# Two graph layers on one core: keys on partitions, unshifted softmax, heads in groups of the array, two batches woven

**Chip, cores, metric.** One core of one Trainium2 chip. The metric is the device time in microseconds of one execution of the whole program; less is better. Engines: PE is TensorE, PEld its weight loads, DVE VectorE, ACT ScalarE, POOL GpSimd.

## The reference, cut

Sixteen graphs of N = 1024 nodes and D = 256 features. The adjacency is 0 or 1 with about 3% ones, although layer 0 accepts edge types 1 to 5.

```python
# layer 0: 4 heads x 64, logits chosen by edge type
h = einsum('bnd,hde->bhne', x, W)
for t in range(5):
    weight += (adj == t + 1) * (e_src[:, :, t, :, None] + e_dst[:, :, t, None, :])
weight = where(adj == 0, -1e9, leaky_relu(weight, 0.01))
dst = einsum('bhij,bhje->bhie', softmax(weight), h) + bias
x = layernorm(x + head_layernorm(relu(dst) + h))
# layer 1: 8 heads x 32, self-attention over the edges, then an MLP 256 -> 1024 -> 256
q = layer_norm(x)                                 # queries, keys and values alike
scores = where(adj > 0, einsum('bhqd,bhkd->bhqk', q, q) / sqrt(32), -inf)
y = x + einsum('bhqk,bhkd->bhqd', softmax(scores), q)
x = layernorm(x + y + gelu(layer_norm(y) @ W1 + b1) @ W2 + b2)
```

## The kernel before

Queries lie on partitions. A head's logits for 128 queries form a 128 x 1024 tile; its row maximum falls out of the masking pass, the exponential gives the row sum, and then the weights must be turned over on PE, 128 x 128 at a time, since a product contracts over partitions and the values have keys there. The cuts are marked `...`.

```python
def logits0(k, hd, es3, ed3, mt, neg0, sums):        # layer 0, 128 queries, one head
    w = two.tile([P, N], F32, name="w")
    for t in range(T):                               # five edge types
        e = ps_s.tile([P, N], F32, name="ps")
        for n in range(NH):
            nc.tensor.matmul(e[:, cols], sel[:, r : r + 1].to_broadcast(...), ed3[:, cols], ...)
            nc.tensor.matmul(e[:, cols], es3[:, ...], sel[:, r : r + 1].to_broadcast(...), ...)
        ...
            nc.vector.copy_predicated(w, mt[:, t, :], e)
    ...
    nc.vector.tensor_tensor_reduce(p, p, neg0, 1.0, -3e38, OP.add, OP.max, mx)
    nc.scalar.activation(p, p, AF.Exp, bias=nmx, scale=1.0, accum_out=sums[:, hd : hd + 1])

def logits1(k, hd, nT, neg1, sums, mxs):             # layer 1: 32 of 128 array rows in use
    c, q = divmod(hd * HD, P)
    for n in range(NH):
        nc.tensor.matmul(s[:, cols], nT[q : q + HD, c, k * P : (k + 1) * P], nT[q : q + HD, c, cols], ...)
    ...

def turn(k, hd):                                     # both layers: weights to keys on partitions
    for q in range(BPH):
        nc.tensor.transpose(pt[:, q, :], p[:, j * P : (j + 1) * P], ident)
    nc.scalar.copy(pT[:, g * BPH : (g + 1) * BPH, :], pt)

def products(k, hd):                                 # both layers: 32 or 64 columns per weight load
    for j in range(NB):
        nc.tensor.matmul(acc[k][:, hd, :], pT[:, j, :], values[:, j, ...], ...)
```

The three stages are woven over the heads, but batches run strictly one after the other.

## Time and profile before

| | before |
|---|---|
| time, median of 3 runs | 17754.5 us (17746.7 to 17767.2) |
| one batch, 17751.8 / 16 | 1109 us |
| PE busy / mean granted clock | 88% / 0.618 |
| DVE, ACT, POOL busy | 41%, 22%, 25% |

A high share of busy PE is not a full array: PE counts as busy while a product uses 32 of its 128 rows, or runs at half clock.

### The profile page before, as it was taken

Reading aid. Unit: us, or ns where it says so; the run is one execution under the profiler, and the core shown is the slowest. Engines: PE = TensorE matmul, PEld = TensorE weight load, DVE = VectorE, ACT = ScalarE, POOL = GpSimd, SP = SyncE. Lnnn points to the kernel's source line nnn. Section 1 sums busy time; section 2 is a strip of 40 time slices with the busy share of each in tenths; the row PEclk is TensorE's granted clock in tenths of the full one; section 3 lists DMA queues with packets and bytes.
Section 4 is the critical chain, followed back from the end, with each engine's and each line's share of the span. In section 5 each row is a group of like instructions: output and inputs, shape, how many; then the busy total and the mean of one; then the engine's idle time right before and its main releaser. Section 6 shows DMA issues by size and latency. Waiting matters only on the chain.

```text
span 17751.8 us, 142034 instructions
## 1 busy us (share of the span) xinstructions
PE 15601.4 (88%) x56064; PEld 10318.6 (58%) x56064; DVE 7284.9 (41%) x12747; ACT 3990.1 (22%) x6880; POOL 4354.5 (25%) x2950
## 2 busy tenths in 40 slices
PE   7988979889798897988979889798897988979889
PEld 4655646556465564655646556465574655646556
DVE  6245162451624516245162451624516245162441
ACT  1222212222122221221212222122221221212222
POOL 5123041230412304123041230412304123041220
PEclk7566575665756657566575665756657566575665
DMA  0000000000000000000000000000000000000000
GB/s 25 3 8 8 3 10 3 8 8 3 10 3 8 8 4 9 3 8 8 4 9 3 8 8 4 9 3 8 7 5 8 3 9 6 4 9 0 9 2 3
DMA packets 59372, 113.19 MB, mean 6 GB/s; under 512 B 7249, under 2 KB 42065, under 8 KB 58705
## 3 DMA queue, kind: packets, MB, share of 16 engines
q1 hardware_dynamic: 53504, 100.68, 1.7%
q8 instruction: 442, 7.24, 0.2%
q10 hardware_dynamic: 5200, 3.42, 0.1%
q14 instruction: 226, 1.84, 0.0%
HBM read 87.31 MB, written 16.78 MB: 6 GB/s over the span
## 4 chain that ended last, share of the span: by engine, by line
PE 68%; POOL 14%; DVE 14%; issue 3%; DMA 1%; ACT 1%; ACTq 0%; DVEq 0%; POOLq 0%
PE po L367 21%; PE ps L298 20%; PE pt L386 14%; DVE w L260 7%; POOL mt L231 6%; PE ps L247 3%; PE ps L250 3%; PE po L347 2%; PE ps L339 2%; POOL neg L233 2%; DVE w L258 2%; POOL neg L234 1%; DMA ak<-in_adj_dram 1%; POOL na L160 1%; POOL o L286 1%
## 5 line engine op out<-in xcount | busy, mean ns | idle before, releaser
L247 PE MATMUL ps<-ed,sel 96*128 96x512 bf16 x5120 | 2589.7, 506 | 1601.8 <-DVE mv L153 530.7
L303 DVE CUSTOM_DVE_ANT_0 p<-ps,neg 128x1024 f32<-128x1024 f32 x1024 | 1253.7, 1224 | 6374.6 <-PE ps L298 6374.6
L367 PEld LDWEIGHTS po<-nrm,pT 128*128 128x128 f32 x16384 | 3562.1, 327 | 200.8 <-issue 200.8
L298 PE MATMUL ps<-fT 32*128 32x512 f32 x4096 | 3617.9, 1089 | 28.5 <-DVE mxs L303 21.1
L367 PE MATMUL po<-nrm,pT 128*128 128x32 f32 x16384 | 3497.3, 387 | 0.0
L386 PEld LDWEIGHTS pt<-ident,p 128*128 128x128 f32 x12288 | 2409.2, 219 | 1652.2 <-issue 1377.3
L387 ACT COPY pT<-pt 128x512 f32<-128x512 f32 x3072 | 1772.9, 585 | 6423.3 <-PE pt L386 6421.5
L260 DVE COPY_PREDICATED w<-mt,ps 128x1024 f32<-128x1024 uint8 x2048 | 2644.5, 1291 | 1136.6 <-PE ps L250 1109.4
L386 PE MATMUL pt<-ident,p 128*128 128x128 f32 x12288 | 2918.2, 413 | 81.1 <-ACT p L267 80.8
L250 PE MATMUL ps<-sel,es 96*128 96x512 bf16 x5120 | 2584.9, 505 | 0.0
L231 POOL TENSOR_SCALAR mt<-ak 128x1024 uint8<-128x1024 int32 x640 | 1772.9, 2784 | 2535.1 <-DVE w L260 2511.8
L250 PEld LDWEIGHTS <-es 96*128 96x128 bf16 x5120 | 625.2, 122 | 2346.7 <-issue 2186.8
L322 POOL TENSOR_TENSOR o<-o,x 128x256 f32<-128x256 f32 x128 | 92.8, 725 | 7614.6 <-DVE nmx L305 7531.5
L298 PEld LDWEIGHTS ps<-fT 32*128 32x128 f32 x4096 | 1062.3, 313 | 942.6 <-issue 813.8
L367 PEld LDWEIGHTS po<-h,pT 128*128 128x128 f32 x8192 | 1368.0, 240 | 209.8 <-ACT pT L387 77.2
L267 ACT ACTIVATE p<-p,nmx 128x1024 f32<-128x1024 f32 x512 | 588.2, 1149 | 3674.9 <-DVE nmx L266 3667.7
L367 PE MATMUL po<-h,pT 128*128 128x64 f32 x8192 | 1317.0, 318 | 0.3 <-ACT pT L387 0.3
L306 ACT ACTIVATE p<-p,nmx 128x1024 f32<-128x1024 f32 x1024 | 1177.3, 1150 | 237.8 <-DVE nmx L305 236.4
L247 PEld LDWEIGHTS <-sel 96*128 96x128 bf16 x5120 | 680.6, 133 | 936.5 <-issue 533.4
L145 POOL TENSOR_TENSOR r<-v,mhalf 128x1 f32<-128x1 f32 (+1 forms) x640 | 427.7, 668 | 1926.5 <-DVE v L143 1905.9
L262 DVE SCALAR_TENSOR_TENSOR p<-w 128x1024 f32<-128x1024 f32 x512 | 734.2, 1434 | 17.7
L264 DVE CUSTOM_DVE_ANT_0 p<-p,neg 128x1024 f32<-128x1024 f32 x512 | 710.6, 1388 | 1.1
(90 smaller groups left out, 7645.9 us busy)
## 6 DMA issues: line engine op xcount, KB each, us to landing
ak<-in_adj_dram SPq DMA_DIRECT2D x128, 512.0 KB, 3.6
xb<-in_x_dram SPq DMA_DIRECT2D x16, 1024.0 KB, 5.3
out_dram<-z SPq DMA_DIRECT2D x128, 128.0 KB, 1.7
w_sb<-in_L_gnn_W_dram ACTq DMA_DIRECT2D x2, 1024.0 KB, 8.3
w_sb<-in_L_gnn_W_dram ACTq DMA_DIRECT2D x2, 128.0 KB, 6.4
g_r<-in_L_gnn_gamma_dram ACTq DMA_DIRECT2D x2, 128.0 KB, 6.7
be_r<-in_L_gnn_beta_dram ACTq DMA_DIRECT2D x2, 128.0 KB, 6.6
bias_r<-in_L_gnn_bias_dram ACTq DMA_DIRECT2D x1, 128.0 KB, 6.3
```

Source lines behind the costliest of these rows:

```text
L231: nc.gpsimd.tensor_scalar(mt[:, t, :], ak, float(t + 1), None, op0=OP.is_equal)
L247: nc.tensor.matmul(e[:, cols], sel[:, r : r + 1].to_broadcast([3 * G, P]), ed3[:, cols], start=True, stop=False)
L250: nc.tensor.matmul(e[:, cols], es3[:, k * P : (k + 1) * P], sel[:, r : r + 1].to_broadcast([3 * G, HALF]), start=False, stop=True,)
L260: nc.vector.copy_predicated(w, mt[:, t, :], e)
L262: nc.vector.scalar_tensor_tensor(p, w, 0.01, w, op0=OP.mult, op1=OP.max)
L264: nc.vector.tensor_tensor_reduce(p, p, neg0, 1.0, -3e38, OP.add, OP.max, mx)
L298: nc.tensor.matmul(s[:, cols], nT[q : q + HD, c, k * P : (k + 1) * P], nT[q : q + HD, c, cols], start=True, stop=True)
L303: nc.vector.tensor_tensor_reduce(p, s, neg1[:, k, :], SCALE1, -3e38, OP.add, OP.max, mx)
L306: nc.scalar.activation(p, p, AF.Exp, bias=nmx, scale=1.0, accum_out=sums[:, hd : hd + 1])
L367: nc.tensor.matmul(acc[k][:, hd, :], pT[:, j, :], values[:, j, hd * width : (hd + 1) * width], start=j == 0, stop=j == NB - 1,)
L386: nc.tensor.transpose(pt[:, q, :], p[:, j * P : (j + 1) * P], ident)
L387: nc.scalar.copy(pT[:, g * BPH : (g + 1) * BPH, :], pt)
```

## The change

Its intent: weights come into being with keys already on partitions, so nothing is turned over; the row sum comes out of the value products; nothing is shifted by a maximum, since a test of the data allows that; heads share the array by groups of 32 rows or columns; and layer 1 of one batch is emitted together with layer 0 of the next. It is nearly a rewrite, so the diff is cut to its core.

```diff
-    # selector products, copy_predicated per type, masked max, Exp with row sum, transposes
+    def layer0(b):                                   # keys on partitions
+        for hd in range(H0):
+            acc = ps([P, NH, HALF], "z")
+            for j in range(NB):
+                g = ring.tile([P, N], F32, name="g")
+                nc.vector.scalar_tensor_tensor(      # the whole weight: max(al, gam) * adj^T
+                    g, al[:, hd, :], gam[:, j, hd : hd + 1], at[:, j, :], op0=OP.max, op1=OP.mult)
+                for n in range(NH):                  # 64 values and a column for the row sum
+                    nc.tensor.matmul(acc[: HO + 1, n, :], ha[:, j, hd, :], g[:, ...], ...)
+                yield
+            ...                                      # divide, relu, residual, norm of the head
+    def layer1(b):
+        def scores(n, c, j):
+            pair = [ps([P, 2, HALF]) for _ in range(HC // 2)]
+            for hh in range(HC):                     # 4 heads in 4 row groups
+                q = hh * HD
+                nc.tensor.matmul(pair[hh // 2][:, hh % 2, :],
+                    nT[q : q + HD, c, j * P : (j + 1) * P], nT[q : q + HD, c, cols], start=True, stop=False)
+            for hh in range(HC):                     # adds -32768 where no edge is
+                nc.tensor.matmul(pair[hh // 2][:, hh % 2, :], negI, zt[:, j, cols], start=False, stop=True)
+            ...
+                nc.scalar.activation(w, s, AF.Exp, scale=SCALE1)
+        def values(acc, c, j, ws):
+            for part in range(2):                    # 4 values, then 4 row sums, in 4 column groups
+                for hh in range(HC):
+                    nc.tensor.matmul(acc[hh * HD : (hh + 1) * HD, part, :],
+                        nrm[:, j, f : f + HD] if part == 0 else ones, ws[hh // 2][:, hh % 2, :], ...)
+        ...                                          # norm, MLP, final norm, for each half of the queries
+    for b in range(B):
+        gens = [(layer1(b), 1)]
+        if b + 1 < B:
+            gens.append((layer0(b + 1), 1))
+        weave(*gens)                                 # one step of each in turn
+        if b + 2 < B:
+            weave((prepare(b + 2), 1))               # adjacency and x transposed, h, exponentials
+    ...
+    with tc.If(failed > 0):                          # tests of adjacency and logits failed
+        general_path(inner)                          # the old method
```

A **step** below is one turn of layer 1's inner loop: four scores, four mask products, two exponentials, four values and four row sums, all for one block of 128 keys, one half of the queries and four heads. A batch has 32. The order in which PE executes is set when the program is built: a scheduler may place an instruction that was emitted later into a place where the earlier ones are still waiting.

## The prediction

> **What bounds the kernel now.** I read the page's busy shares and clock first, then a table by stage of one batch (16 alike, 17751.8 / 16 = 1109 us each), then the groups kept apart by shape, then the timeline of TensorE inside a stage.
>
> ```profile
> PE 15601.4 (88%) x56064; PEld 10318.6 (58%) x56064; DVE 7284.9 (41%) x12747; ACT 3990.1 (22%) x6880; POOL 4354.5 (25%) x2950
> PEclk7566575665756657566575665756657566575665
> PE 68%; POOL 14%; DVE 14%; issue 3%; DMA 1%; ACT 1%; ACTq 0%; DVEq 0%; POOLq 0%
> ```
>
> PE is busy 88% of the time and holds 68% of the chain that ended last, at a granted clock of 0.5 to 0.7. Bytes do not matter (6 GB/s).
>
> ```profile
> 499.50:1082.00 582.50, 557.53 (x1802) 393.16 (x1802) 114.74 (x293) 152.86 (x267) 53.15 (x53) 0.50 0.01 2
> 100.00:499.50 399.50, 310.16 (x1244) 186.54 (x1243) 276.76 (x407) 69.06 (x119) 200.71 (x117) 0.66 0.03 8
> 1082.00:1150.00 68.00, 66.39 (x249) 44.96 (x248) 14.82 (x46) 14.86 (x26) 18.28 (x16) 0.94 0.09 30
> ```
>
> Columns: stretch, length, then busy us of PE, PEld, DVE, ACT, POOL, and the clock. The first is layer 1's attention: PE 96% busy, clock 0.50 throughout. The second is layer 0's: PE 78% and DVE 69% busy, trading waits. The third is the MLP and the next batch's preparation, at 0.94.
>
> ```profile
> L298 PE MATMUL ps<-fT 32*128 32x512 f32 x4096 | 3617.9, 1089 | 28.5 <-DVE mxs L303 21.1 <-ACT fT L168 7.4
> L367 PE MATMUL po<-nrm,pT 128*128 128x32 f32 x16384 | 3497.3, 387 | 0.0
> L386 PE MATMUL pt<-ident,p 128*128 128x128 f32 x12288 | 2918.2, 413 | 81.1 <-ACT p L267 80.8
> L250 PE MATMUL ps<-sel,es 96*128 96x512 bf16 x5120 | 2584.9, 505 | 0.0
> L194 PE MATMUL ps<-fT,w_sb 128*128 128x512 f32 x256 | 112.5, 592 | 0.0
> L262 DVE SCALAR_TENSOR_TENSOR p<-w 128x1024 f32<-128x1024 f32 x512 | 734.2, 1434 | 17.7
> L306 ACT ACTIVATE p<-p,nmx 128x1024 f32<-128x1024 f32 x1024 | 1177.3, 1150 | 237.8 <-DVE nmx L305 236.4
> L315 DVE RECIPROCAL rinv<-edge 128x8 f32<-128x8 f32 x128 | 26.0, 203 | 4.4
> L272 DVE RECIPROCAL rinv<-sums 128x4 f32<-128x4 f32 x128 | 21.5, 168 | 21.9 <-ACT p L267 21.9
> ```
>
> For matmuls divide busy time by count (means contain the pipeline's tail). L298's loop makes 2048 products but leaves 4096 records: a float32 matmul is two passes. A float32 pass of 512 columns takes 112.5/256 = **0.44 us** at full clock (L194) and 3617.9/4096 = **0.88 us** at half (L298); I call the first T. A bf16 matmul of 512 takes 0.505 at mixed clock, so I take half of T, 0.22, at full clock. A float32 transpose takes 2918.2/12288 = 0.24 us.
>
> ```profile
> 801.05 3.78 PE L298 MATMUL ps<-fT 32*128 32x512 f32 x4
> ```
>
> The four passes of one head's scores fill 3.78 us one after another, on 32 of 128 rows. Bursts of this kind are longer than a clock window yet never raised the clock in 582 us, whereas a run of 128-row float32 products did within microseconds of the MLP's start.
>
> **What the Trainium skill says.** "TensorE: Matmul & The Clock Gate", Part 1: the array runs at half clock until activity in a window of about 3.4 us releases it; the trace agrees on the two levels (0.50, 1.00; T doubles). Same page, Part 3: matmuls on different row or column groups overlap, but matmuls keep strict order. The kernel before has no neighbouring products in different groups, so its trace shows nothing of this. "TensorEngine Tiling (Array Packing)", Key Properties: changing the tiling mode drains the array; not visible before either, layer 1's sums leave room for about 0.1 us a switch. "VectorE: DVE Perf Modes", First, the fixed hardware budget: reciprocal is iterative, repeat count 8; the rows agree: (203 - 168)/4 = 8.75 ns per element against about 1.1 for other work.
>
> **The change, part by part** (per batch, full clock).
>
> *Removed.* All 768 weight transposes and their 1773 us of copies on ACT; the narrow products (L367, 32 or 64 columns per weight load, 3497 + 1317 us); all 640 selector products (5175 us); DVE's five predicated passes and masked maxima; GpSimd's masks. These are most of 15601 us of PE. The general path is a branch not taken for this data (edges 0/1, small logits): I charge it nothing.
>
> *Layer 1, added.* 32 steps (2 query halves, 2 head groups, 8 key blocks), each with 4 float32 scores on four row groups, 4 bf16 mask products over the whole array, and 8 float32 value products (4 values, 4 row-sum replicas by ones) on four column groups, 512 columns each. Serial this is 8T + 2T + 16T = 26T. With overlap and strict order the two passes of one product still follow each other on their own group, and the next product's first pass can run only beside the previous one's second: n products take n + 1 passes. So 5T + 2T + 9T = 16T = 7.0 us; four mode switches make **7.3 us** (estimate). Times 32: 234 us, against 582 before. Two Exps of 1.15 us per step on ACT hide under 7.3 us.
>
> *Layer 0.* 64 float32 products of 512 columns (K 128, M 65): 64 x 0.88 = 56 us, woven beside layer 1 but on the same PE, so it adds. Its DVE pass is 32 x 1.43 = 46 us, hidden.
>
> *MLP.* 64 products of 512: 56 us, much as before. *Transposes* of results, norms and MLP output: 96 x 0.24 = 23 us.
>
> *Waits.* Layer norm before each MLP is a DVE chain of 10 to 18 us (reciprocal of 512 elements alone about 4.5 us); the first has layer 0 steps beside it, the second has none left: 8 + 14 us. Each head end of layer 0 copies its one PSUM accumulator out before the transposes: 4 x 2 us. Together 30 us (estimate).
>
> *Preparation* is emitted after the woven stretch, not in it. Eight adjacency loads through two buffers, 64 bf16 transposes, 2048-element copies on ACT (about 2 us), an 8192-element ACT pass of about 8 us that the built order puts between the two x^T copies, 16 products of 264 columns (32 passes x 0.24) and 16 of 512 (14 us): 57 us, half of it PE.
>
> *Sum:* 234 + 56 + 56 + 23 + 30 + 57 = 456 us. Fifteen of these 6840; last batch without layer 0 and preparation about 340; prologue about 200 (one preparation, and layer 0 of batch 0 with nothing woven). **About 7400 us.** DVE comes to some 145 us a batch, ACT 125: neither binds.
>
> **Rivals.**
> *The clock stays at half.* If activity is counted by cells in use, the steps (two groups of four at a time, 65 columns of 128 in layer 0) keep the array about half used, and 0.50 could persist as in layer 1 before. For it: the K=32 bursts that never raised the clock. Against: values and layer 0 use all 128 rows, and the built order keeps them back to back for 13T. Steps and layer 0 would double: 456 + 234 + 56 = 746, about **11000 us**.
> *Full overlap:* if passes of all four groups run at once, a step is 2T + 2T + 4T = 3.5 us; 456 - 122 = 334 a batch, about **5500 us**. Against it: the strict order.
> *No overlap* for two-pass products, 26T = 11.4 us: 587 a batch, about **9500 us** at full clock, beyond 15000 at half. Against: the order of instructions is plainly written for overlap, and the ones products would make no sense serially.
> *Waits win:* head tails on DVE's in-order queue (about 7 us of small work each), the norm chains and a preparation slowed by the casting loads could add 50 us a batch, about **8200 us**.
>
> **Range and chances.** I give the strict-order overlap 0.6, full overlap 0.2, none 0.2, and a clock mostly at full 0.65. The median lies a little above 7400 because most errors lengthen it: **7800 us**. The range, 5600 to 11600, goes from full overlap to half clock with strict order. Even no overlap at half clock would only approach 17754. Faster by over 2%: 0.98; within 2%: 0.01; slower: 0.01.
>
> **What would show it.** Right: about 450 us per batch; a woven step of about 9 us (7.3 + two layer 0 products); score passes in neighbouring row groups starting about T apart, pairwise overlapping; clock above 0.9 in woven stretches; some 50 to 60 us of half-idle PE between them; DVE under 40%. Wrong: a clock near 0.5 in woven stretches; four scores starting together or eight passes strictly in line; DVE or ACT ending most of PE's waits inside steps; preparation much over 60 us.

## The result

| | before | after |
|---|---|---|
| time, median of 4 runs each | 17760.85 us | 5627.2 us (5621.9 to 5631.7) |
| ratio | | 0.3168 (0.3163 to 0.3172) |
| PE busy, us | 15601.4 | 4825.3 |
| mean granted clock | 0.618 | 0.911 |

Ratios here and below are the mean time of one kernel's fast runs over that of the other's of the same rounds, so not quite the ratio of the medians. All outputs are right.

The page of the kernel after, the lines of busy time, of the clock over the span in 40 slices, and of the shares of the chain that ended last:

```profile
PE 4825.3 (86%) x22273; PEld 1764.0 (31%) x22273; DVE 2006.9 (36%) x3361; ACT 1836.4 (33%) x1952; POOL 323.0 (6%) x295
PEclk9898998989989899898989989899898998989998
PE 66%; issue 12%; DVE 11%; DMA 5%; ACT 4%; POOL 2%; ACTq 0%; POOLq 0%; DVEq 0%
```

PE still bounds the kernel, but at 0.8 to 0.9 and more of full clock in every slice, with a third of the busy time. GpSimd has left the chain nearly altogether (14% before, 2% now).

Where a batch spends its time, kernel after, two consecutive windows (stretch, length, then busy us of PE, PEld, DVE, ACT, POOL, the clock, the share of DMA and GB/s). The first runs from the start of one batch's woven stretch to its end, the second is the preparation that follows:

```profile
1952.04:2246.62 294.58, 268.02 (x1241) 87.88 (x1240) 112.34 (x184) 90.50 (x100) 14.70 (x9) 0.94 0.02 6
2246.62:2300.20 53.58, 35.08 (x152) 22.86 (x152) 12.61 (x24) 24.28 (x23) 5.38 (x9) 0.71 0.29 49
```

A batch takes 348 us where 456 were predicted. The clock and the preparation (53.6 us against 57) are close to the prediction, so nearly all of the difference of 108 us lies in the woven stretch: 294.6 us against 456 - 57 = 399. One woven step there, timeline of PE (start, duration, line, tile, shape, instructions):

```profile
2310.89 1.14 PE L365 MATMUL ps_s<-nT 32*128 32x512 f32 x8
2311.96 1.04 PE L373 MATMUL ps_s<-zt,negI 128*128 128x512 fp8e4 x4
2312.93 1.07 PE L385 MATMUL ps_a<-w,nrm 128*32 128x512 f32 x8
2313.81 1.04 PE L385 MATMUL ps_a<-w,ones 128*32 128x512 f32 x8
2314.78 1.93 PE L286 MATMUL ps_z<-g,ha 128*65 128x512 f32 x4
```

From start to start, layer 1's own work takes 2314.78 - 2310.89 = 3.9 us, not 7.3, and layer 0's two products (four passes) the expected 1.9. Eight score passes occupy 1.07 us. One pass alone takes T = 0.44, so eight in line would take 3.5 us and two rounds of four at once 0.88. The same row in the kernel before needed 3.78 us for four passes in line, at half clock.

Cut still finer, windows that count only the score products (length, PE busy, matmul records of the window, then the same of the weight loads and the clock):

```profile
2310.90:2311.00 0.10, 0.10 (x4) 0.10 (x5) 1.00 0.00 0
2311.40:2311.60 0.20, 0.20 (x8) 0.00 (x0) 1.00 0.00 0
```

Four records are in flight within the first tenth of a microsecond, and some 0.5 us later eight touch one window: the first four ending, the second four beginning. That is four heads side by side, twice, which the prediction had listed under "wrong".

Groups of instructions of the kernel after, from the page (busy us, mean ns of one, idle time before them and what ended it):

```profile
L365 PE MATMUL ps_s<-nT 32*128 32x512 f32 x4096 | 681.3, 645 | 15.7 <-ACT w L377 13.8
L385 PE MATMUL ps_a<-w,nrm 128*32 128x512 f32 x4096 | 545.0, 604 | 0.0
L286 PE MATMUL ps_z<-g,ha 128*65 128x512 f32 x2048 | 1029.3, 633 | 99.6 <-DVE g L282 60.5
L445 PE MATMUL ps_s<-fT,w_sb 128*128 128x512 f32 x1024 | 529.0, 651 | 44.7 <-ACT hid L452 25.9
L456 PE MATMUL ps_a<-hid,w_sb 128*128 128x512 f32 x1024 | 460.3, 592 | 0.0
L406 DVE RECIPROCAL den<-ps_a 128x512 f32<-128x512 f32 x64 | 214.8, 3356 | 311.9 <-PE ps_a L385 311.9
L377 ACT ACTIVATE w<-ps_s 128x1024 f32<-128x1024 f32 x1024 | 995.4, 1020 | 1520.9 <-PE ps_s L373 1520.9
```

The scores are the same 4096 passes as before: 3617.9 us then, 681.3 now. A factor of two of that is the clock, the rest is the four row groups. Only 13.8 us of PE's waits before them are for an exponential, so the exponentials hide. Per batch, layer 0's products take 1029.3 / 16 = 64 us and the MLP (529.0 + 460.3) / 16 = 62 us, together as much as the 32 steps of layer 1's attention, 32 x 3.9 = 125 us.

What still costs: PE is idle for 5628.2 - 4825.3 = 803 us. Much of it looks like this, the second norm before an MLP, timeline of PE (in brackets the idle time and what ended it):

```profile
2199.41 1.76 PE L416 MATMUL ps_s<-ident,u 128*128 128x128 f32 x7 [0.60 <-DVE u L408]
2210.64 1.97 PE L433 MATMUL ps_s<-ident,t 128*128 128x128 f32 x8 [9.47 <-DVE t L429]
```

PE waits 9.5 us for DVE's norm because no layer 0 product is left; before the first MLP of a batch 16 passes of layer 0, 8.95 us of them, fill the same place. The experiments ask two things: why a step takes 3.9 us, and whether the weaving and the rest of the change pay.

### The profile page after: what moved, and what is told of

Same layout as the page of the kernel before. It is cut to its first block, busy times and chain, and to the rows that moved or that the text cites. A ratio compares the mean times of both kernels' runs of the same rounds, so it can differ in the third digit from the quotient of the medians.

```text
span 5628.2 us, 51957 instructions
## 1 busy us (share of the span) xinstructions
PE 4825.3 (86%) x22273; PEld 1764.0 (31%) x22273; DVE 2006.9 (36%) x3361; ACT 1836.4 (33%) x1952; POOL 323.0 (6%) x295
## 4 chain that ended last, share of the span: by engine, by line
PE 66%; issue 12%; DVE 11%; DMA 5%; ACT 4%; POOL 2%; ACTq 0%; POOLq 0%; DVEq 0%
PE ps_a L385 16%; PE ps_z L286 14%; PE ps_s L365 10%; PE ps_s L373 8%; PE ps_s L445 5%; PE ps_a L456 4%; PE ps_s L262 4%; DMA ab<-in_adj_dram 4%; DVE den L406 3%; PE ps_s L239 2%; ACT zt L272 2%; POOL r L184 1%; DVE st L192 1%; POOL r L320 1%; PE ps_s L216 1%
## 5 line engine op out<-in xcount | busy, mean ns | idle before, releaser
L377 ACT ACTIVATE w<-ps_s 128x1024 f32<-128x1024 f32 x1024 | 995.4, 1020 | 1520.9 <-PE ps_s L373 1520.9
L286 PE MATMUL ps_z<-g,ha 128*65 128x512 f32 x2048 | 1029.3, 633 | 99.6 <-DVE g L282 60.5
L282 DVE SCALAR_TENSOR_TENSOR g<-al,gam,at 128x1024 f32<-128x1024 f32 x512 | 647.3, 1282 | 1302.4 <-PE ps_z L286 1300.1
L365 PE MATMUL ps_s<-nT 32*128 32x512 f32 x4096 | 681.3, 645 | 15.7 <-ACT w L377 13.8
L445 PE MATMUL ps_s<-fT,w_sb 128*128 128x512 f32 x1024 | 529.0, 651 | 44.7 <-ACT hid L452 25.9
L385 PE MATMUL ps_a<-w,ones 128*32 128x512 f32 x4096 | 548.7, 592 | 0.0
L385 PE MATMUL ps_a<-w,nrm 128*32 128x512 f32 x4096 | 545.0, 604 | 0.0
L373 PE MATMUL ps_s<-zt,negI 128*128 128x512 fp8e4 x2048 | 533.9, 382 | 0.0
L286 PEld LDWEIGHTS ps_z<-g,ha 128*65 128x65 f32 x2048 | 266.4, 144 | 782.6 <-issue 675.4
L456 PE MATMUL ps_a<-hid,w_sb 128*128 128x512 f32 x1024 | 460.3, 592 | 0.0
L406 DVE RECIPROCAL den<-ps_a 128x512 f32<-128x512 f32 x64 | 214.8, 3356 | 311.9 <-PE ps_a L385 311.9
L216 PE MATMUL ps_s<-identb,ab 128*128 128x128 bf16 x1024 | 113.2, 279 | 214.1 <-DMA ab<-in_adj_dram 182.2
```

What stands on the lines that cost most here:

```text
L282: nc.vector.scalar_tensor_tensor(g, st["al"][:, hd, :], st["gam"][:, j, hd : hd + 1], st["at"][:, j, :], op0=OP.max, op1=OP.mult)
L286: nc.tensor.matmul(acc[: HO + 1, n, :], st["ha"][:, j, hd, :], g[:, n * HALF : (n + 1) * HALF], start=j == 0, stop=j == NB - 1,)
L365: nc.tensor.matmul(pair[hh // 2][:, hh % 2, :], nT[q : q + HD, c, j * P : (j + 1) * P], nT[q : q + HD, c, cols], start=True, stop=False,)
L373: nc.tensor.matmul(pair[hh // 2][:, hh % 2, :], negI, zt[:, j, cols], start=False, stop=True)
L377: nc.scalar.activation(w, s, AF.Exp, scale=SCALE1)
L385: nc.tensor.matmul(acc[hh * HD : (hh + 1) * HD, part, :], nrm[:, j, f : f + HD] if part == 0 else ones, ws[hh // 2][:, hh % 2, :], start=j ...
```

## The experiments

| run | edit, against | median us | ratio to before |
|---|---|---|---|
| e1_values_by_group | values and sums head by head | 5636.8 | 0.3171 |
| e2_scores_serial | each score followed by its mask | 8421.9 | 0.4738 |
| e3_unwoven | layers emitted one after the other | 5353.4 | 0.3011 |
| e4_prepare_woven | preparation woven too | 5925.0 | 0.3332 |
| e5_sums_on_dve | e3, row sums gathered by DVE | 5464.8 | 0.3075 |
| e6_four_adj_buffers | e3, 4 adjacency buffers | 5359.4 | 0.3015 |
| e7_no_general_path | branch left out | 5621.3 | 0.3164 |
| e8_weave_two_to_one | two steps of layer 1 to one of layer 0 | 5347.9 | 0.3008 |
| e9_x_early_adj4 | e8 + e6 + x loaded in pieces | 5329.1 | 0.3002 |
| e10_sums_on_dve_two_to_one | e5 + e8 | 5318.2 | 0.2996 |
| e11_sums_dve_x_early | e10 + x loaded in pieces | 5259.3 | 0.2962 |

Intervals of the ratios are within 0.0007 of the values shown, of e2's within 0.0013.

### e1: does the order across groups bind?

The theory of the prediction, strict order, allows overlap only between neighbouring products in different groups. Its rival: each group goes through its own products in order and knows nothing of the others. If strict order holds, putting a head's values and sums next to each other, both in the same group, must cost much.

```diff
-                for part in range(2):
-                    for hh in range(HC):
+                for hh in range(HC):
+                    for part in range(2):
```

> The eight value products of a step are issued group by group (values of head 0, ones of head 0, values of head 1, ...) instead of first the values of all four column groups, then the ones. Same products, same result. T is one float32 pass of 512 columns, 0.44 us; in the changed kernel the sixteen passes take 4T = 1.77 us. Theory G (a product waits until its own column group is free, and no later product starts before it): head 1's first product starts together with head 0's second, so the eight products take five product times, 10T = 4.4 us; 2.6 us more in each of 512 steps, about 6980 us. Theory R (the single passes keep a strict order, and only the passes of neighbouring products on different groups were put side by side): 13T = 5.7 us, about 7660 us. Theory Q (each group has its own queue): nothing changes, about 5630 us.

Measured: 5636.8 us against 5627.2, no difference worth a name. One could suspect that the scheduler undid the edit. The order of the built program goes nrm (the values), ones (the row sums), nrm, ones through the four heads. For this text the kernel of e1 was built once more; the instructions compiled for PE stand in that order too, with the two passes of a product next to each other. The trace shows another order. Windows of e1, first those of the ones products alone, then those of the nrm products alone (length, PE busy, records, weight loads, DVE, clock):

```profile
2311.50:2311.90 0.40, 0.00 (x0) 0.10 (x4) 0.00 (x0) 1.00 0.00 0
2311.90:2312.20 0.30, 0.00 (x0) 0.06 (x4) 0.00 (x0) 1.00 0.00 0
2312.20:2312.50 0.30, 0.27 (x4) 0.15 (x4) 0.00 (x0) 1.00 0.00 0
```

```profile
2311.30:2311.50 0.20, 0.15 (x4) 0.15 (x8) 0.00 (x0) 1.00 0.00 0
2311.50:2311.90 0.40, 0.40 (x8) 0.03 (x2) 0.00 (x0) 1.00 0.00 0
```

All four heads' nrm products start within 0.2 us, though three of them stand behind a ones product in the program, and no ones product runs before 2312.2, 0.9 us later, when its own group is free. So a product waits for its own group, not for earlier products of other groups. That settles the step: scores 2T, masks 2T, values and sums 4T, together 3.52 us, and the switches between groups of rows, the whole array and groups of columns. Why the chip lets the groups run apart is not something these runs show.

### e2: one group at a time

```diff
                     )
-                for hh in range(HC):
                     nc.tensor.matmul(pair[hh // 2][:, hh % 2, :], negI, zt[:, j, cols], start=False, stop=True)
```

A mask product uses all 128 rows and now stands between any two scores; in the timeline below each score runs alone.

> Each head's score product is followed at once by its full-array mask product, so that no two score products can overlap. Same products, same result. If the overlap of the four row groups is what made the steps short: scores take 8T instead of 2T, 2.6 us more, and six more switches of mode at about 0.1 us, so 3.2 us more in each of 512 steps, about 7290 us. If the waits on ScalarE and VectorE set the steps and the overlap was worth little: under 6000 us. The granted clock should fall below the 0.91 of the changed kernel if a single 32-row group counts as little activity, and stay if any streaming counts.

Measured: 8421.9 us, 2795 more than after, a good deal beyond what was expected. The direction shows that the overlap of the row groups is what made the scores cheap: the scores' busy time went from 681.3 to 2654.2 us, in the page of e2:

```profile
L365 PE MATMUL ps_s<-nT 32*128 32x512 f32 x4096 | 2654.2, 731 | 0.0
```

The size needs a second cause. Timeline of PE in e2, a score and its mask product, at two places:

```profile
3408.80 1.12 PE L365 MATMUL ps_s<-nT 32*128 32x512 f32 x2
3409.86 0.39 PE L372 MATMUL ps_s<-zt,negI 128*128 128x512 fp8e4 x1
...
3427.54 2.07 PE L365 MATMUL ps_s<-nT 32*128 32x512 f32 x2
3429.54 0.61 PE L372 MATMUL ps_s<-zt,negI 128*128 128x512 fp8e4 x1
```

From its start to the next start the same pair takes 1.38 us at 3408 and 2.54 us at 3427. Windows of one microsecond, during the first pair and after the last pair of its step (length, busy us of the engines, clock):

```profile
3409.00:3410.00 1.00, 1.00 (x3) 0.19 (x2) 1.00 (x1) 0.00 (x0) 0.00 (x0) 1.00 0.00 0
3415.00:3416.00 1.00, 1.00 (x12) 0.36 (x8) 0.00 (x0) 0.48 (x1) 0.00 (x0) 0.50 0.00 0
```

PE is busy in every microsecond, yet some 5.5 us after single scores and masks began at 3408.8 the clock drops to 0.50 for some 3 us, and the values that run then take nearly twice as long: over the whole run nrm and ones together go from 1094 to 1694 us. The delay is not a constant: singles begin again at 3422.2, the clock falls 2.7 us later and stays at 0.50 for some 10 us. The mean clock is 0.798 against 0.911. So products on 32 of 128 rows, one at a time with masks between them, do not hold the clock up here (whether the few rows or the many switches matter was not separated), which fits the scores of the kernel before, at 0.50 throughout. The prediction's worry that half-used arrays might keep the clock down was right for one row group alone and wrong for four at once.

### e3: does the weaving pay?

```diff
-            weave(*gens)
+            for g in gens:
+                weave(g)
```

> Layer 1 of a batch and layer 0 of the next are emitted one after the other instead of woven. If the weave hides the waits (Exp of ScalarE behind only 1.8 us of value products, about 0.7 us exposed in 32 steps; four head ends of layer 0 at about 9 us; the norm of layer 0, 20 us; the first norm before the MLP, 10 us): about 90 us more per batch, about 7000 us, and a lower clock. If the matmuls set the time wherever they stand: under 5950 us.

Measured: 5353.4 us, 5% **faster** than the woven kernel. That lies within the second theory's "under 5950", but neither theory had foreseen a gain. Timeline of PE in e3, around the second norm before an MLP, the place shown above for the kernel after:

```profile
2042.55 6.17 PE L286 MATMUL ps_z<-g,ha 128*65 128x512 f32 x14
...
2061.33 1.09 PE L433 MATMUL ps_s<-ident,t 128*128 128x128 f32 x8 [0.22 <-DVE t L429]
```

And one line of its view of waits (total us, times, longest):

```profile
PE ps_s L433 <- DVE t L429: 20.4, 6, 9.6
```

Layer 0's products (L286) now stand where the norm before an MLP made PE wait: its wait is 0.22 us here (between the lines left out PE waits 5 us for layer 0's own head end). The group "PE waits for DVE's t" falls from 161 us in 17 waits to 20 us in 6. The scheduler puts layer 0 there by itself, because emitted after layer 1 it is taken only where layer 1 has nothing ready. The weave of one to one did the opposite: it spent layer 0 in steps that PE fills without help: counted from mask to mask in the traces, 384 steps of e3 hold no layer 0 product and take 3.89 us (median), and 240 steps of the kernel after hold two and take 5.76, so the two cost their full 1.87 us there. The count closes: PE's idle time goes from 803 to 678 us (span 5349.8 less 4671.6 busy), and its busy time falls by 154 us for the same 22273 instructions; 125 + 154 = 279 us is the difference of the two spans. The mean clock rises from 0.911 to 0.929, which by itself would take 4825 x (1 - 0.911 / 0.929) = 93 us off the busy time (estimate); what the rest is was not separated.

### e8: half the weave

This tests the reading of e3 from the other side. If layer 0 is worth most as filler, two steps of layer 1 to one of layer 0 should leave enough of it for the second norm.

```diff
-            gens = [(layer1(b), 1)]
+            gens = [(layer1(b), 2)]
```

> The changed kernel with the weave at two steps of layer 1 to one of layer 0, so that half of layer 0 is left when the second norm and MLP of layer 1 come. Theory of the filler (layer 0 is worth most beside the norms and the start of the next preparation, and the one-to-one weave has used it up by then, in steps that TensorE fills anyway): close to the version emitted layer by layer, 5350 to 5450 us. Rival (the gain of that version is from something else, as fewer changes of shape inside the steps): between, 5480 to 5600 us.

Measured: 5347.9 us, as e3. The wait for DVE's t is down to 19 us in 2 waits. The filler theory stands.

### e4: weave the preparation as well

Preparation takes 54 us per batch at a clock of 0.71, a third of it idle. Emitted with layer 0 of its batch beside layer 1 of the one before, it might hide.

```diff
+        def ahead(b):
+            yield from prepare(b)
+            yield from layer0(b)
...
-                gens.append((layer0(b + 1), 1))
+                gens.append((ahead(b + 1), 1))
             weave(*gens)
-            if b + 2 < B:
-                weave((prepare(b + 2), 1))
```

It also needed a buffer of its own for the MLP's input, and for that room layer 0 got three buffers for its weights in place of four.

> The preparation of the next batch is woven beside layer 1 as well, ahead of its layer 0 (its own buffer for the MLP's transposed input; three instead of four buffers for g to make room). In the changed kernel the preparation stands alone, 53 us per batch of which TensorE idles about 20. If those idle times are filled: 15 x 20 = 300 us less, about 5330 us. If the preparation takes the two PSUM buffers of the scores and stalls them as much as it saves: 5550 to 5700 us.

Measured: 5925.0 us, 5% **slower** than after. Timeline of PE in e4:

```profile
2008.43 0.72 PE L350 MATMUL ps_z<-ident,nrm 128*128 128x128 f32 x2 [22.15 <-DVE nrm L344]
...
2025.55 1.13 PE L366 MATMUL ps_s<-nT 32*128 32x512 f32 x4 [0.46 <-ACT at L218]
```

Two things go wrong. The end of layer 0, its norm, now has nothing beside it, and PE waits 22 us for it. And the preparation takes the two PSUM buffers of the scores: in the second line the scores wait for ACT's copy of an adjacency tile, and only four of the eight passes are there. Both show in the totals: PE's waits for nrm go from 26.6 us in the kernel after to 404.7, the scores' busy time from 681.3 to 893.8 us, while the waits for adjacency loads nearly go (from 182.2 to 10.4). How the net 298 us divide, and what the three buffers cost, was not separated.

### e5, e10: row sums by DVE

The ones products repeat the same sum 32 times over. DVE, at 37%, can add the weights over the eight key blocks, so that one round of ones products replaces eight. e5 does so on e3, e10 on e8's weave. Layer 0's weights had to go down to two buffers.

```diff
+            def add(wsum, before, ws, j):
+                for i in range(HC // 2):
+                    nc.vector.tensor_add(wsum[:, i], before[i] if j == 1 else wsum[:, i], ws[i])
...
                         if before is not None:
+                            add(wsum, before, ws, j)
                             values(acc, c, j - 1, before)      # 4 values only
...
+                    sums(acc, wsum)                            # 4 ones products, once
```

> Built on the version emitted layer by layer (5353 us). VectorE adds the exponentials of the eight key blocks (two additions of 1024 columns, about 1.22 us each by the rows of that shape, in 7 of 8 steps), and one round of ones products replaces eight. TensorE loses 7/8 of the 533 us of ones products, 466 us; a step falls from 3.9 to 3.0 us, and the additions (2.4 us) fit beside it. If TensorE still sets the end: 4890 to 5000 us. If VectorE's in-order queue (then some 3070 us busy) becomes the wait, because layer 0's g and the norms stand behind the additions: above 5200 us. It also has two buffers for g instead of four, to make room.

Measured: 5464.8 us, 2% slower than e3. A step should have lost 0.97 us; it went from 3.9 to 3.69. Timeline of PE in e5, one step:

```profile
2036.12 1.04 PE L374 MATMUL ps_s<-zt,negI 128*128 128x512 fp8e4 x4
2037.09 1.06 PE L385 MATMUL ps_a<-w,nrm 128*32 128x512 f32 x8
2038.08 1.80 PE L366 MATMUL ps_s<-nT 32*128 32x512 f32 x8
```

The scores now spread over 1.80 us instead of 1.14. In the view of waits, their weight loads wait for ACT's exponentials, which free the scores' two PSUM buffers:

```profile
PEld ps_s L366 <- ACT w L378: 547.6, 879, 1.2
PE ps_s L230 <- DMA xb<-in_x_dram: 313.8, 15, 21.1
```

(total us, times, longest.) ACT's two exponentials of this step run from 2036.76 to 2038.70, and the second pair of scores starts at 2038.75. Masks, two exponentials one after the other, then the next scores: this round takes 3.69 us (the median of 384 steps), and most of the ones products' 0.97 us had stood in its shadow. The total of the first line alone would not show that: it is 403.3 us in e3 too, whose steps lose nothing by it. The second line is work that e5 no longer hides, the load of x: 169.8 us in e3. The median time lies in the range of the rival, DVE's queue, and layer 0's weights do come late (82.0 us of PE's waits; e3 lists none); whether DVE's additions or the two buffers cause this was not separated.

> Row sums on VectorE as in the earlier run, but with the two-to-one weave. Theory (without the ones products a step of 3.0 us of TensorE work is shorter than the round from masks through two Exps back to the score buffers, 3.7 us; layer 0 products fill it in every second step): 0.2 us saved in one half of the steps and 0.9 in the other, 5348 - 280 = about 5070, up to 5150 us. Rival (VectorE's additions delay g and the norms, whatever stands in the steps): above 5350 us.

Measured: 5318.2 us, ratio 0.2996 against 0.3008 of e8, so 0.4% faster and far short of what was expected. Steps with two layer 0 products take 4.90 us (5.76 in e8), those without 3.69 (3.89 in e8), so a filled step does save the 0.9 us expected. But the trace has only 105 such filled steps of 512, not half: the scheduler puts most of layer 0 elsewhere. In the other steps the exponentials still hold the scores back (the scores' busy time is 884.3 us against 682.5 in e8), PE waits 175.6 us for x (115.5 in e8), and layer 0's weights now come late from a DVE that is 57% busy (205.0 us of waits by weight loads, 111.5 by products).

### e6, e9, e11: the loads of the preparation

In e3 PE still waits 165 us for adjacency tiles and 170 us for x. e6 gives the adjacency four buffers for two (and layer 0's weights three for four). e9 adds the weave of e8 and loads x in two halves where they are used, and again per head for the residual, so that its buffer no longer has to be held until layer 0 ends. e11 is e10 with x loaded that way.

```diff
-            xb = st["xb"] = one.tile([P, NB, D], F32, name="xb")
-            nc.sync.dma_start(xb, x[b].rearrange("(k p) d -> p k d", p=P))
...
             for c in range(DC):
+                xb = one.tile([P, NB, P], F32, name="xb")
+                nc.sync.dma_start(xb, x[b].rearrange("(k p) d -> p k d", p=P)[:, :, c * P : (c + 1) * P])
...
             for hd in range(H0):
+                xh = two.tile([P, NB, HO], F32, name="xh")
+                nc.sync.dma_start(xh, x[b].rearrange("(k p) d -> p k d", p=P)[:, :, hd * HO : (hd + 1) * HO])
```

> Built on the version emitted layer by layer (5353 us): four buffers for the adjacency loads instead of two (three for g instead of four). There TensorE idled 165 us until such a load had landed. If those waits end the preparation: 100 to 150 us less, about 5230 us. If other waits stand close behind them (the load of x, the copies of ScalarE, the 7 us pass over zt): 5320 to 5350 us.

> The two-to-one weave (5348 us) with both loads of the preparation made early: four buffers for the adjacency blocks, and x loaded in two halves for the transposes and again per head for the residual, so that no load waits until layer 0 has used x up (the run with four adjacency buffers alone gained nothing: the wait for x grew from 170 to 318 us). If the loads are what the preparation waits for: the 160 us for adjacency and 115 us for x go, 5100 to 5200 us. If ScalarE's copies and the pass over zt stand behind them: 5280 to 5350 us.

> The run before with x loaded in halves and again per head. In the version with sums on VectorE emitted layer by layer TensorE idled 314 us for x. If that wait is real and nothing stands behind it: 100 to 250 us below the run before. If the adjacency loads, still in two buffers, end the wait: within 40 us of it.

Measured: e6 5359.4 us, nothing gained on e3; e9 5329.1, which by the ratios (0.3002, 0.2997 to 0.3007, against 0.3008, 0.3003 to 0.3013, on another chip) is not told apart from e8; e11 5259.3, 59 less than e10 on the same chip, and the best of all. One line of the view of waits of e6:

```profile
PE ps_s L231 <- DMA xb<-in_x_dram: 317.8, 15, 21.7
```

With the adjacency early (its wait falls from 165 to 6.8 us), PE comes to x sooner and waits for that: 317.8 us instead of 170. In e9 both waits are lower than in e8, from which it differs (x 97 us after 115.5, adjacency 68.4 after 162.4), but the end of layer 0's norm holds up the transposes behind it: 101.6 us by products (44.0 in e8) and 118.4 by weight loads (39.6). Against e10, e11 halves the wait for x (82.7 us after 175.6); the adjacency, with only two buffers, stays (128.1 after 134.2). Each cure moves PE to the next thing that is late. What would remain if all of them were cured at once was not tried.

### e7: is the branch free?

```diff
-    failed = nc.values_load(bad_i[0:1, 0:1], min_val=0, max_val=1)
-    with tc.If(failed > 0):
-        with ExitStack() as inner:
-            general_path(inner)
```

> The changed kernel without the general path and its branch (the tests are still computed). The prediction charged the branch nothing: 5605 to 5630 us against 5627. If the path not taken costs anything (code to fetch, constants kept): over 1% less, under 5570 us.

Measured: 5621.3 us (5611 to 5630) against 5627.2 (5622 to 5632): ratios 0.3164 (0.3159 to 0.3169) and 0.3168 (0.3163 to 0.3172), not told apart. The branch that is not taken costs nothing measurable.

## Why the prediction was right or wrong

The time, 5627 us, lies just inside the range of 5600 to 11600 and the direction was given 0.98; but the reckoning of 7400 was 1800 us too long, and nearly all of it is one term. That the range holds the result, by 27 us, is no merit of the mechanism believed in: its lower end had been set for the rival with full overlap.

**The failed step** is "with overlap and strict order ... n products take n + 1 passes", which made a step 5T + 2T + 9T = 16T, 7.3 us with its switches. The runs show 2T + 2T + 4T = 8T, 3.5 us, and 3.9 with the switches: e1 shows that the order across groups does not bind, e2 that the overlap is real. In a batch this is 32 x (7.3 - 3.9) = 109 us, and the batch came out at 348 in place of 456, so 108 us short. The rival called "full overlap" had this step, without switches, and came to 5500 us, 2% from the result; it was given 0.2 against 0.6, on the strength of a rule read, although the kernel before showed nothing of it either way and the order in which the change was written (all four heads, then all four masks) argued for overlap of whole products as well as for strict order.

**Right, with small differences of size.**
- PE remains the bound, and the exponentials (1.02 us each) and layer 0's DVE pass hide. DVE is at 36%, under the 40% stated.
- The clock: above 0.9, given 0.65. e2 shows that the risk was real: with the same products issued one group at a time the mean clock is 0.798.
- Layer 0: 1.87 us a step (the next step starts at 2316.65), 32 of them 60 us, against 56. MLP: 62 us against 56. Preparation: 53.6 against 57. Waits in the woven stretch: 294.6 - 268.0 = 26.6 us idle against 30.
- Transposes: (62.9 + 49.0 + 42.0 + 64.8 + 46.9) / 16 = 17 us against 23. The 0.24 us for one were a mean of the kernel before, over stages at lowered clocks, and were used as a time at full clock.
- The reciprocal of 512 columns: 3.36 us, not 4.5. The 8.75 ns per element were taken from the difference of two tiny rows; at full length it is 3356 / 512 = 6.6 ns with all fixed cost in it.
- Switches of mode: layer 1's 3.89 us against 8T = 3.52 leave 0.37 us over three changes, layer 0's 1.87 against 4T = 1.76 leave 0.11 with the fourth. That is some 0.12 us each, if nothing else lies in it (estimate), against 0.1; how the 0.1 had been worked out is not shown.
- The general path: no measurable cost (e7).

**A sum that is wrong, without effect on the result.** The rival with half the clock gives 746 us a batch, so 15 x 746 = 11190 us, and with the last batch and the prologue, doubled in the same way, about 12000: above the 11000 stated and above the end of the range.

**Not foreseen.** That "layers of two batches woven", a part of the change that the prediction took for a plain gain, costs 5% against emitting them one after the other (e3). The prediction saw the sign of it, "the second has none left: 8 + 14 us", but counted it as a wait of the change and did not ask whether the weave itself used up what would have filled it.

**Still open.** How far the kernel can go once loads, layer 0's norm chain and DVE are all out of the way; e11 at 5259 us, 6.5% below the kernel after by the ratios (0.2962 / 0.3168), is the best that was run, not a floor.

## What to carry to other kernels

Where products have few rows or columns, put them in groups side by side and reckon with the groups' own times: the longest queue in one group decides, not the sum and not the order across groups. Count also what it does for the clock, since a busy PE with one group of 32 rows in use may run at half speed. And work of another batch is filler: give it to the places where the first one waits, by emitting it later, not evenly; then check in the waits what has become late in its place.

## What the Trainium skill lacked or had wrong

- "TensorE: Matmul & The Clock Gate", Part 3, states that matmuls keep program order in start and in end. e1 differs: the sums that stand second in the program start 0.9 us after the values that stand third, fifth and seventh, and the time is unchanged (5637 against 5627 us). The part also has no case of float32, where a product is two passes: eight such passes in four row groups take 1.07 us here against 8 x 0.44 = 3.52 us in line, 3.3 times faster.
- The same page, Part 1, ties the clock to how busy PE has been. In e2 PE was busy in every microsecond looked at, and the clock still fell to 0.50, 5.5 us and again 2.7 us after single products on 32 rows with masks between them had begun; in the kernel after, with four row groups together, it stood at 1.00 in the step shown. Beyond a remark on transposes (Part 4), which products count as activity is missing.
- "TensorEngine Tiling (Array Packing)", Key Properties, says that tiles operate independently, which e1 bears out against the other page, and that a change of mode drains the array, without a figure: about 0.12 us each here (estimate; 3.89 us hold 3.52 us of passes and three changes).
- "VectorE: DVE Perf Modes", First, the fixed hardware budget, names the iterations of the reciprocal but no time: 3.36 us for 128 x 512 here.
